# Softplus summed in PSUM, and a part of GpSimd's multiplies given to VectorE, in a selective-scan kernel

## The chip, the cores and the metric

The kernel runs on one core of one Trainium2 chip. The metric is the device time of one execution in microseconds (us). TensorE is called PE in the profile, VectorE DVE, ScalarE ACT, GpSimd POOL and SyncE SP; SP only issues DMAs here.

## The reference, cut to what matters

Two layers work on 16 images of 64 x 64 pixels with 96 channels, in float32. The first is a convolution block (upsample, two matrix multiplies with a quadratic between, low-pass filter). The second, in which the change lies, is a selective scan in four directions over L = 4096 pixels, 192 channels and 16 states:

```python
delta = jax.nn.softplus(dts + dt_bias[None, :, :, None])
...
def step(h, inps):
    dt, ut, bt, ct = inps
    h = jnp.exp(dt[..., None] * As[None]) * h + (dt * ut)[..., None] * bt[:, :, None, :]
    y = jnp.einsum('bkdn,bkn->bkd', h, ct)
    return (h, y)
```

So for each channel and state there is a decay exp(delta A), a drive delta u B, the recurrence h = decay h + drive along the pixels, and a sum of h C over the 16 states.

## The kernel before, in words

All work is issued in an order written out by hand: each engine executes its instructions in the order in which the program emits them, and waits for others by semaphores.

**The main loop** (`scan`, from L833) runs over 3072 units: 16 images x 8 steps (two pairs of directions, four stretches of T = 1024 pixels) x 6 blocks of 64 channels x 4 quarters j of the states. Partitions hold 32 channels x 4 states; each unit has two groups, odd (e = 1) and even (e = 0), of 128 x 1024 elements. A unit n does this:

- `decay(n, e)`, L725: ACT writes da = exp(delta A) to PSUM (two buffers `aps`). It is issued a unit ahead.
- `drive(n)`, L731: POOL writes b = dtu x B for both groups at once into a buffer of the pool `p3` (three of them). It is issued two units ahead.
- `recur(n, e)`, L740 (forward) and L742 (backward): DVE scans h = da h + b. For the odd group the result overwrites b in SBUF, for the even group it overwrites da in PSUM.
- Multiply by C: for the odd group POOL, in place in b (L877); for the even group DVE, from da in PSUM into b (L887).
- `keep(n, e)`, L748: ACT copies the last column of h, 128 x 1, which starts the next stretch. The last stretch of a direction needs none, so there are 2304 copies for each group.
- `read_out(n)`, L764: PE sums b over the states into y in PSUM with sixteen recorded matmuls. It is issued in unit n + 1, so that the buffer b is free for drive(n + 3). At the end of a block `store` (L775) copies y out of PSUM. For the second pair of directions a partial sum y0 is loaded (L702) and added by PE (L757).

In the order of the program a unit is: odd scan, odd keep, odd decay for n + 1, read_out(n - 1), background slot 0, odd multiply on POOL, drive(n + 2) on POOL, even scan, slot 1, even multiply, even keep, even decay for n + 1, slot 2, then loads of B and C (L693).

**Background work** is cut into slices by generators and one slice of each running generator is put into a slot: `project` for the next step (L622), `front` for the next image (the first layer and the convolution, L181), and `finish` for the image before (L510). `project` makes, for each half of 512 pixels and each of three parts v, softplus in the form max(s, 0) + ln(1 + e) with a correction for the rounding of 1 + e, where e = exp(-|s|): in L658 to L674 that is ACT abs, ACT exp, ACT ln, DVE max-add (L664), ACT 1 + e (L666), DVE (1 + e) - 1 - e (L668), DVE subtract (L669), DVE dtu = delta u (L672) and ACT copy of delta (L674); dtu and delta go to DRAM (L676, L677). There are 768 such parts in the run. s lies in the one bank of the PSUM pool `gps`. The blocks load dtu and delta back, spread over the partitions, with `fetch` (L684), each as one tile with both groups and two buffers.

Of the kernel before, what the change touches and what calls it, by code (L numbers as in the profile page):

```python
# [45 lines left out]
F32 = mybir.dt.float32  # L46
AF = mybir.ActivationFunctionType
ALU = mybir.AluOpType
# [3 lines left out]
C = 96  # L52
HW = 64
L = HW * HW
UPS = 100
# [7 lines left out]
T = 1024  # L63
NT = L // T
NQ = 4
QT = T // NQ
TB = 512
# [6 lines left out]
HEAVY = 2  # L74
PSLICES = 60


@with_exitstack
def tile_two_blocks(
# [4 lines left out]
    nc = tc.nc  # L84
# [27 lines left out]
    one_s = const.tile([128, 1], F32, name="one_s")  # L112
    nc.gpsimd.memset(one_s, 1.0)
    eps_g = const.tile([128, 1], F32, name="eps_g")
    nc.gpsimd.memset(eps_g, GEPS)
# [66 lines left out]
    b18 = ctx.enter_context(tc.tile_pool(name="b18", bufs=1))  # L182
    b12 = ctx.enter_context(tc.tile_pool(name="b12", bufs=1))
    b2p = ctx.enter_context(tc.tile_pool(name="b2", bufs=11))
# [55 lines left out]
    def front(mi):  # L240
# [72 lines left out]
        for p0 in range(0, UPS, PP):  # L313
# [93 lines left out]

        JS = 44
        s = [
            b18.tile([UPS, JS, C], F32, name="s0", tag="b18"), b12.tile([UPS, HW - JS, C], F32, name="s1", tag="b12")  # L410
        ]
        for _ in range(2):
            yield
        for i, n, first in [(0, JS // 4, k * JS // 4) for k in range(4)] + [(1, 10, 0), (1, 10, 10)]:
            nc.sync.dma_start(out=s[i][:, first:first + n, :], in_=s_d[:, JS * i + first:JS * i + first + n, :])
            yield
# [3 lines left out]
        done = None  # L420
        for j0 in range(0, HW + 8, 8):
            if done is not None:
                nc.scalar.activation(
                    x1v[:, :, j0 - 8:j0], done.rearrange("c w h -> c h w"), AF.Identity, bias=shift
                )
            if j0 < HW:
                done = bank([C, 8, HW], "e_ps")
                nc.tensor.matmul(
                    done.rearrange("c w h -> c h w"), lhsT=lin, rhs=x1v[:, :, j0:j0 + 8], start=True, stop=False,
                    skip_group_check=True,  # L430
                )
                for j in range(8):
                    nc.tensor.matmul(
                        done[:, j, :], lhsT=s[(j0 + j) // JS][:, (j0 + j) % JS, :], rhs=down_s, start=False, stop=True,
                        skip_group_check=True,
                    )
            yield
# [168 lines left out]
    def scan():  # L606


        with ExitStack() as es:
            pj = es.enter_context(tc.tile_pool(name="sc_pj", bufs=1))  # L610
            up_ = es.enter_context(tc.tile_pool(name="sc_u", bufs=3))
            cp = es.enter_context(tc.tile_pool(name="sc_bc", bufs=5))
            p3 = es.enter_context(tc.tile_pool(name="sc_3", bufs=3))
            p2 = es.enter_context(tc.tile_pool(name="sc_2", bufs=2))
            yp = es.enter_context(tc.tile_pool(name="sc_y", bufs=1))
# [6 lines left out]
            def project(mi, pair, lc, out):  # L622
# [5 lines left out]
                out["dtu"] = [dram.tile([128, T], F32, name=f"dtu_d{v}") for v in range(3)]  # L628
                xs_d = image[mi]["xs"]
                for t in range(0, T, TB):  # L630
                    u = []
                    for v in range(3):
                        uv = up_.tile([128, TB], F32, name="u")
                        nc.sync.dma_start(out=uv, in_=xs_d[v, :, lc * T + t:lc * T + t + TB])
                        u.append(uv)
                    for _ in range(3):
                        yield
                    pp = gps.tile([128, TB], F32, name="pp", tag="g")
                    for v in range(3):
                        nc.tensor.matmul(pp, lhsT=xpt_s[:, pair, v, :], rhs=u[v], start=(v == 0), stop=(v == 2))  # L640
                    yield
                    pr = pj.tile([128, TB], F32, name="pr")
                    nc.scalar.activation(pr, pp, AF.Identity, bias=bumps_s)


                    for i, v in enumerate((0, 2, 1)):
                        if i == 0:
# [8 lines left out]
                        yield  # L656
                        e, d = (pj.tile([128, TB], F32, name=k) for k in ("e", "d"))
                        nc.scalar.activation(e, s, AF.Abs)  # L658
                        nc.scalar.activation(e, e, AF.Exp, scale=-1.0)
                        yield  # L660
                        nc.scalar.activation(d, e, AF.Ln, bias=one_s)
                        for _ in range(2):
                            yield
                        nc.vector.scalar_tensor_tensor(d, s, 0.0, d, ALU.max, ALU.add)  # L664
                        yield
                        nc.scalar.activation(s, e, AF.Identity, bias=one_s)  # L666
                        yield
                        nc.vector.scalar_tensor_tensor(s, s, -1.0, e, ALU.add, ALU.subtract)  # L668
                        nc.vector.tensor_sub(s, d, s)  # L669
                        dtu = pj.tile([128, TB], F32, name="dtu")  # L670
                        delta = pj.tile([128, TB], F32, name="delta")
                        nc.vector.tensor_mul(dtu, s, u[v])  # L672
                        yield
                        nc.scalar.copy(delta, s)  # L674
                        yield
                        nc.sync.dma_start(out=out["dtu"][v][:, t:t + TB], in_=dtu)  # L676
                        nc.sync.dma_start(out=out["delta"][v][:, t:t + TB], in_=delta)  # L677

            def fetch(what, ctx, bi):

                v, s0, r = blocks[bi]
                t = p2.tile([128, 2, T], F32, name=what)
                for e in (1, 0):
                    nc.sync.dma_start(  # L684
                        out=t[:, e, :],
                        in_=ctx[what][v][32 * (s0 + e):32 * (s0 + e) + 32, :].unsqueeze(1).to_broadcast([32, NQ, T]),
                    )
                return t
# [22 lines left out]
            bc = {(what, 0, j): fetch_bc(ctxs[0], 0, j, what) for j in range(NQ) for what in range(2)}  # L711
            ops = {(w, 0): fetch(w, ctxs[0], 0) for w in ("dtu", "delta")}
            y0s, states, ys = {}, [None] * len(blocks), {}
# [8 lines left out]
            def decay(n, e):  # L722
                k, g = group(n, e)
                da = aps.tile([128, T], F32, name="da")
                nc.scalar.activation(da, ops["delta", n // NQ][:, e, :], AF.Exp, scale=a_s[:, k, g, units[n][2]:units[n][2] + 1])  # L725
                das[n, e] = da

            def drive(n):
                b = p3.tile([128, 2, T], F32, name="b")
                bt = bc[0, blocks[units[n][1]][2], units[n][2]]  # L730
                nc.gpsimd.tensor_mul(b, ops["dtu", n // NQ], bt.unsqueeze(1).to_broadcast([128, 2, T]))  # L731
                bs[n] = b
# [10 lines left out]

            def keep(n, e, h):
                st, bi, j = units[n]
                if st % NT < NT - 1:
                    end = h[:, T - 1:T] if steps[st][1] == 0 else h[:, 0:1]
                    nc.scalar.copy(states[bi][1][:, e, j:j + 1], end)  # L748

# [83 lines left out]
            for n, (st, bi, j) in enumerate(units):  # L833
# [19 lines left out]
                if j == 0:  # L853
# [6 lines left out]
                    if ahead:  # L860
                        ops["dtu", m + 1] = fetch("dtu", *ahead)
                elif j == 1:
                    if ahead:
                        ops["delta", m + 1] = fetch("delta", *ahead)
                    if n + NQ <= last and steps[units[n + NQ - 1][0]][1] == 1:
                        st2, bi2, _ = units[n + NQ - 1]
                        y0s[steps[st2][2], bi2] = fetch_y0(steps[st2][2], bi2)

                h = bs[n][:, 1, :]
                recur(n, 1, h)  # L870
                keep(n, 1, h)
                if n < last:
                    decay(n + 1, 1)
                if n:
                    read_out(n - 1)
                slot(0)
                nc.gpsimd.tensor_mul(h, h, bc[1, r, j])  # L877
                if n + 2 <= last:
# [3 lines left out]
                recur(n, 0, h)  # L882
                if n and units[n - 1][2] == NQ - 1:
                    storing = store(n - 1)
                    next(storing)
                slot(1)
                nc.vector.tensor_mul(bs[n][:, 0, :], h, bc[1, r, j])  # L887
                keep(n, 0, h)
                if n < last:
                    decay(n + 1, 0)  # L890
                slot(2)
                if storing is not None:
                    next(storing, 0)
                    storing = None


                at = n % per_step
                for what in range(2):
# [4 lines left out]
                    if 0 <= ahead_j < NQ and st + 1 < len(steps):  # L903
                        bc[what, 0, ahead_j] = fetch_bc(ctxs[st + 1], 0, ahead_j, what)
            read_out(last)
            for _ in store(last):
# [111 lines left out]
```

## Time and profile before

The columns come from the run's times and the page of one profiled execution.

| what | value |
|---|---|
| time, median of 3 runs | 21,918.01 us (21,916.37 to 21,922.08) |
| profiled execution, its own time | 21,910.69 us |
| its span in the profile | 21,908.9 us |
| mean granted TensorE clock | 0.766 of full speed |
| mean DMA rate | 195 GB/s, DMA engines busy 58.1% of the span for the main queue |
| one execution's work | 260,666 instructions |

How to read it: a busy time is the time in which an engine executed something, summed over the span. A share of it is a mean over all stages. In a group of instructions, "mean ns" is the duration of one, and the idle time is that of the engine just before these instructions, with what ended most of it. In the waits, "y L764 <- DVE b L887" means that the instruction on y at line 764 was released last by the DVE instruction at line 887 that wrote b.

### The profile page before, as it was taken

How to read it: one execution, taken by the hardware profiler on the slowest of the kernel's cores; microseconds unless marked ns; L12 is line 12 of the kernel's file. 1: busy time of each engine (PE TensorE's matmuls, PEld its weight loads, DVE VectorE, ACT ScalarE, POOL GpSimd, SP SyncE). 2: the span in 40 equal slices, each digit the busy share in tenths (PEclk: the TensorE clock that was granted, in tenths of full speed). 3: DMA queues.
4: the chain of work that ended last, by engine and by line, in shares of the span. 5: the costliest groups of instructions: out<-in, count | busy, mean ns of one | idle time of the engine just before them, and what ended most of it. 6: DMA issues, size and time to landing. Idle time of an engine off the chain costs nothing.

```text
span 21908.9 us, 260666 instructions
## 1 busy us (share of the span) xinstructions
PE 15342.2 (70%) x92844; PEld 6324.7 (29%) x92844; DVE 19849.9 (91%) x12829; ACT 13130.2 (60%) x20854; POOL 20900.4 (95%) x6152
## 2 busy tenths in 40 slices
PE   6766767766777677777767677767777677677745
PEld 4322323232232322324233232322323223242211
DVE  0999999999999999999999999999999999999996
ACT  4665656666565665656656566665656656566543
POOL 0999999999999999999999999999999999999997
PEclk7776777877778777777877778777787877778856
DMA  2555565656656566565655656556565655656654
GB/s 80 190 191 188 193 214 194 209 195 200 205 191 215 189 206 201 192 215 192 207 198 194 214 192 209 196 201 206 193 211 189 210 199 198 206 195 208 210 177 134
DMA packets 1851895, 4276.30 MB, mean 195 GB/s; under 512 B 449118, under 2 KB 548350, under 8 KB 1848542
## 3 DMA queue, kind: packets, MB, share of 16 engines
q1 hardware_dynamic: 1850590, 4259.62, 58.1%
q8 instruction: 731, 11.98, 0.2%
q14 instruction: 574, 4.70, 0.1%
HBM read 3380.58 MB, written 878.18 MB: 194 GB/s over the span
## 4 chain that ended last, share of the span: by engine, by line
DVE 36%; POOL 19%; issue 18%; PE 9%; ACT 9%; DMA 7%; SPq 1%; POOLq 0%; DVEq 0%; ACTq 0%
POOL b L731 10%; POOL b L877 10%; DVE da L742 7%; DVE da L740 7%; DVE b L740 6%; DVE b L742 6%; DVE b L887 4%; ACT da L725 4%; DMA u<-xs_d 2%; DVE s L669 2%; DVE dtu L672 2%; DVE s L668 2%; PE y L764 1%; DMA ct<-rows 1%; PE pp L640 1%
## 5 line engine op out<-in xcount | busy, mean ns | idle before, releaser
L731 POOL TENSOR_TENSOR b<-dtu,bt 128x2048 f32<-128x2048 f32 x3072 | 13984.9, 4552 | 584.6 <-DMA dtu<-dtu_d 522.9
L725 ACT ACTIVATE da<-delta,a_s 128x1024 f32<-128x1024 f32 x6144 | 6853.5, 1116 | 2826.6 <-DVE b L887 1185.9
L877 POOL TENSOR_TENSOR b<-b,ct 128x1024 f32<-128x1024 f32 x3072 | 7309.1, 2379 | 259.8 <-ACT new L748 249.5
L764 PE MATMUL y<-b,fold_s 128*32 128x256 f32 x49152 | 4638.9, 492 | 4107.3 <-DVE b L887 3102.6
L887 DVE TENSOR_TENSOR b<-da,ct 128x1024 f32<-128x1024 f32 x3072 | 3752.6, 1222 | 84.5
L764 PEld LDWEIGHTS y<-b,fold_s 128*32 128x32 f32 x49152 | 1353.3, 126 | 7627.7 <-DVE b L887 4083.3
L740 DVE TENSOR_TENSOR_SCAN da<-da,new,b 128x1024 f32<-128x1024 f32 x1152 | 2694.3, 2339 | 252.3 <-ACT da L725 252.3
L740 DVE TENSOR_TENSOR_SCAN b<-da,new,b 128x1024 f32<-128x1024 f32 x1152 | 2698.0, 2342 | 174.1 <-POOL b L731 166.9
L742 DVE TENSOR_TENSOR_SCAN da<-da,new,b 128x1024 f32<-128x1024 f32 x1152 | 2693.8, 2338 | 172.9 <-ACT da L725 172.7
L742 DVE TENSOR_TENSOR_SCAN b<-da,new,b 128x1024 f32<-128x1024 f32 x1152 | 2697.1, 2341 | 151.6 <-POOL b L731 109.5
L748 ACT COPY new<-da 128x1 f32<-128x1 f32 x2304 | 362.3, 157 | 3028.5 <-DVE b L887 3023.2
L473 PE MATMUL c_ps<-xgp,wtap_s 96*128 96x512 f32 (+1 forms) x4608 | 1817.8, 675 | 168.9 <-ACT row L491 164.1
L650 PE MATMUL s<-pr,dtw_s 128*128 128x512 f32 x1536 | 1120.4, 819 | 557.8 <-ACT delta L674 516.7
L377 PE MATMUL o_ps<-w2c_s,hsq 128*100 128x96 f32 x9600 | 1205.3, 293 | 191.9 <-ACT hsq L348 180.1
L365 PE MATMUL h_ps<-xu,w1t_s 96*128 96x500 f32 x1920 | 1147.6, 700 | 244.2 <-ACT hsq L348 108.6
L748 ACT COPY new<-b 128x1 f32<-128x1 f32 x2304 | 432.6, 188 | 1445.7 <-DVE b L742 740.4
L377 PEld LDWEIGHTS o_ps<-w2c_s,hsq 128*100 128x100 f32 x9600 | 1119.5, 203 | 407.4 <-ACT hsq L348 227.7
L640 PE MATMUL pp<-u,xpt_s 128*128 128x512 f32 x1536 | 903.7, 734 | 224.2 <-DMA u<-xs_d 216.0
L742 DVE TENSOR_TENSOR_SCAN b<-da,b 128x1024 f32<-128x1024 f32 x384 | 876.7, 2283 | 133.2 <-ACT da L725 74.8
L473 PEld LDWEIGHTS c_ps<-xgp,wtap_s 96*128 96x128 f32 (+1 forms) x4608 | 631.9, 182 | 1193.3 <-issue 938.6
L740 DVE TENSOR_TENSOR_SCAN da<-da,b 128x1024 f32<-128x1024 f32 x384 | 875.8, 2281 | 106.9 <-ACT da L725 106.9
L742 DVE TENSOR_TENSOR_SCAN da<-da,b 128x1024 f32<-128x1024 f32 x384 | 876.0, 2281 | 105.0 <-ACT da L725 105.0
(120 smaller groups left out, 18077.1 us busy)
## 6 DMA issues: line engine op xcount, KB each, us to landing
dtu<-dtu_d SPq DMA_DIRECT2D x1536, 512.0 KB
delta<-delta_d SPq DMA_DIRECT2D x1536, 512.0 KB
bt<-rows SPq DMA_DIRECT2D x1024, 512.0 KB
ct<-rows SPq DMA_DIRECT2D x1024, 512.0 KB
u<-xs_d SPq DMA_DIRECT2D x896, 256.0 KB
dtu_d<-dtu SPq DMA_DIRECT2D x768, 256.0 KB
delta_d<-delta SPq DMA_DIRECT2D x768, 256.0 KB
xr<-in_x SPq DMA_DIRECT2D x768, 128.0 KB
```

The costliest lines, as they stand in the source:

```text
L365: nc.tensor.matmul(h_ps[j], lhsT=w1t_s[:, 128 * j:128 * (j + 1)], rhs=xu.rearrange("c p q -> c (p q)"), start=True, stop=True,)
L377: nc.tensor.matmul(o_ps[:, p, :], lhsT=hsq[j][:, UPS * p:UPS * (p + 1)], rhs=w2c_s[:, j, :], start=(j == 0), stop=(j == HB - 1),)
L473: nc.tensor.matmul(c_ps[p:p + n], lhsT=wtap_s[:, tap, 128 * i:128 * i + n], rhs=xgp[:, h0:h0 + 8, dx:dx + HW], start=(tap == 0), stop=(tap ...
L640: nc.tensor.matmul(pp, lhsT=xpt_s[:, pair, v, :], rhs=u[v], start=(v == 0), stop=(v == 2))
L650: nc.tensor.matmul(s, lhsT=dtw_s[:, pair, v, :], rhs=pr, start=True, stop=True)
L725: nc.scalar.activation(da, ops["delta", n // NQ][:, e, :], AF.Exp, scale=a_s[:, k, g, units[n][2]:units[n][2] + 1])
L731: nc.gpsimd.tensor_mul(b, ops["dtu", n // NQ], bt.unsqueeze(1).to_broadcast([128, 2, T]))
L740: nc.vector.tensor_tensor_scan(out, da, b, before, ALU.mult, ALU.add)
L742: nc.vector.tensor_tensor_scan(out[:, ::-1], da[:, ::-1], b[:, ::-1], before, ALU.mult, ALU.add)
L764: nc.tensor.matmul(y[32 * q:32 * q + 32, e, :], lhsT=fold_s, rhs=b[:, e, QT * q:QT * q + QT], start=(pair == 0 and j == 0 and e == 0), sto ...
L877: nc.gpsimd.tensor_mul(h, h, bc[1, r, j])
L887: nc.vector.tensor_mul(bs[n][:, 0, :], h, bc[1, r, j])
```

## The change

The change has these parts.

- *Softplus in PSUM.* The three DVE operations L664, L668 and L669 and the ACT operation L666 go. ACT makes m = relu(s), w = (1 + e) and w = w - 1 in SBUF tiles; PE adds -w + e + ln(1 + e) + m in PSUM by four matmuls with the identity or its negative (`less_i`). DVE still makes dtu from it, ACT still copies delta.
- *One odd group in five.* For n % 5 = 4 the odd scan writes its result to da in PSUM, and DVE multiplies it by C into b; POOL's multiply is left out there.
- *Odd column copy.* `keep` of the odd group is issued on DVE instead of ACT, except in those fifth units, where ACT copies from da.
- *Read-out.* `read_out(n)` moves from unit n + 1 to unit n + 2, and b has four buffers (`p4`) in place of three; `store` and the load of y0 move along.
- *Loads.* Delta is fetched by halves into three half buffers (odd half at j = 1, even half at j = 2) in place of two whole ones; u has four buffers and is fetched ahead in `project`; the load of s_d in `front` uses one buffer twice (40 and 24 columns) in place of two buffers (44 and 20), which frees room.

```diff
+SHARE = 5
...
+    less_s = const.tile([128, 1], F32, name="less_s")
+    nc.gpsimd.memset(less_s, -1.0)
+    less_i = const.tile([128, 128], F32, name="less_i")
+    nc.vector.tensor_scalar(less_i, ident_s, -1.0, None, ALU.mult)
...
-    b12 = ctx.enter_context(tc.tile_pool(name="b12", bufs=1))
...
-        JS = 44
-        s = [
-            b18.tile([UPS, JS, C], F32, name="s0", tag="b18"), b12.tile([UPS, HW - JS, C], F32, name="s1", tag="b12")
-        ]
+        def fetch_s(first, n):
+            t = b18.tile([UPS, n, C], F32, name="s", tag="b18")
+            for k in range(0, n, 8):
+                nc.sync.dma_start(out=t[:, k:k + 8, :], in_=s_d[:, first + k:first + k + 8, :])
+                yield t, first
+
+        JS = 40
         for _ in range(2):
             yield
-        for i, n, first in [(0, JS // 4, k * JS // 4) for k in range(4)] + [(1, 10, 0), (1, 10, 10)]:
-            nc.sync.dma_start(out=s[i][:, first:first + n, :], in_=s_d[:, JS * i + first:JS * i + first + n, :])
+        for s, s_first in fetch_s(0, JS):
             yield
...
+            if j0 == JS:
+                for s, s_first in fetch_s(JS, HW - JS):
+                    yield
+                for _ in range(2):
+                    yield
...
-            up_ = es.enter_context(tc.tile_pool(name="sc_u", bufs=3))
+            up_ = es.enter_context(tc.tile_pool(name="sc_u", bufs=4))
...
+            p4 = es.enter_context(tc.tile_pool(name="sc_4", bufs=4))
...
+                order = (0, 2, 1)
+
+                def fetch_u(v, t):
+                    uv = up_.tile([128, TB], F32, name="u")
+                    nc.sync.dma_start(out=uv, in_=xs_d[v, :, lc * T + t:lc * T + t + TB])
+                    return uv
+
+                ahead_u = [fetch_u(v, 0) for v in order]
+                for _ in range(4):
+                    yield
...
-                        e, d = (pj.tile([128, TB], F32, name=k) for k in ("e", "d"))
+                        e, d, m, w = (pj.tile([128, TB], F32, name=k) for k in ("e", "d", "m", "w"))
                         nc.scalar.activation(e, s, AF.Abs)
                         nc.scalar.activation(e, e, AF.Exp, scale=-1.0)
                         yield
+                        nc.scalar.activation(m, s, AF.Relu)
+                        nc.scalar.activation(w, e, AF.Identity, bias=one_s)
+                        yield
                         nc.scalar.activation(d, e, AF.Ln, bias=one_s)
+                        nc.scalar.activation(w, w, AF.Identity, bias=less_s)
+                        yield
+                        s = gps.tile([128, TB], F32, name="s", tag="g")
+                        yield
+                        for k, (sign, of) in enumerate(((less_i, w), (ident_s, e), (ident_s, d), (ident_s, m))):
+                            nc.tensor.matmul(s, lhsT=sign, rhs=of, start=(k == 0), stop=(k == 3))
                         for _ in range(2):
                             yield
-                        nc.vector.scalar_tensor_tensor(d, s, 0.0, d, ALU.max, ALU.add)
-                        yield
-                        nc.scalar.activation(s, e, AF.Identity, bias=one_s)
-                        yield
-                        nc.vector.scalar_tensor_tensor(s, s, -1.0, e, ALU.add, ALU.subtract)
-                        nc.vector.tensor_sub(s, d, s)
...
+                        if t + TB < T:
+                            ahead_u.append(fetch_u(v, t + TB))
...
-                b = p3.tile([128, 2, T], F32, name="b")
+                b = p4.tile([128, 2, T], F32, name="b")
...
-            def keep(n, e, h):
+            def keep(n, e, h, copy):
...
-                    nc.scalar.copy(states[bi][1][:, e, j:j + 1], end)
+                    copy(states[bi][1][:, e, j:j + 1], end)
...
                 elif j == 1:
                     if ahead:
-                        ops["delta", m + 1] = fetch("delta", *ahead)
-                    if n + NQ <= last and steps[units[n + NQ - 1][0]][1] == 1:
-                        st2, bi2, _ = units[n + NQ - 1]
-                        y0s[steps[st2][2], bi2] = fetch_y0(steps[st2][2], bi2)
-
-                h = bs[n][:, 1, :]
+                        deltas[m + 1, 1] = fetch_delta(*ahead, 1)
+
+                odd_here = n % SHARE == SHARE - 1
+                h = das[n, 1] if odd_here else bs[n][:, 1, :]
                 recur(n, 1, h)
-                keep(n, 1, h)
+                if odd_here:
+                    nc.vector.tensor_mul(bs[n][:, 1, :], h, bc[1, r, j])
+                keep(n, 1, h, nc.scalar.copy if odd_here else nc.vector.tensor_copy)
                 if n < last:
                     decay(n + 1, 1)
-                if n:
-                    read_out(n - 1)
+                if j == 2 and ahead:
+                    deltas[m + 1, 0] = fetch_delta(*ahead, 0)
+                if n >= 2:
+                    read_out(n - 2)
                 slot(0)
-                nc.gpsimd.tensor_mul(h, h, bc[1, r, j])
+                if not odd_here:
+                    nc.gpsimd.tensor_mul(h, h, bc[1, r, j])
...
-                if n and units[n - 1][2] == NQ - 1:
-                    storing = store(n - 1)
+                if n >= 2 and units[n - 2][2] == NQ - 1:
+                    storing = store(n - 2)
...
+                if j == NQ - 1 and n < last and steps[units[n + 1][0]][1] == 1:
+                    st2, bi2, _ = units[n + 1]
+                    y0s[steps[st2][2], bi2] = fetch_y0(steps[st2][2], bi2)
```

## The prediction

> **What bounds the kernel now.** I read the first page of the profile, then the groups of instructions by line and shape, the table of who waited for whom, the timeline of a few units in mid-run, and a table of stages. A "unit" below is one turn of the main loop (one block, one quarter j); there are 3072. First the page: span and busy time.
>
> ```profile
> span 21908.9 us, 260666 instructions
> PE 15342.2 (70%) x92844; PEld 6324.7 (29%) x92844; DVE 19849.9 (91%) x12829; ACT 13130.2 (60%) x20854; POOL 20900.4 (95%) x6152
> ```
>
> POOL (GpSimd) and DVE (VectorE) are nearly full. The timeline of one undisturbed unit (start, duration, engine, line, tiles) shows which sets the pace:
>
> ```profile
> 10015.91 2.35 POOL L877 TENSOR_TENSOR b<-b,ct 128x1024 f32<-128x1024 f32 x1
> 10016.86 2.34 DVE L740 TENSOR_TENSOR_SCAN b<-da,new,b 128x1024 f32<-128x1024 f32 x1
> ...
> 10018.22 4.53 POOL L731 TENSOR_TENSOR b<-dtu,bt 128x2048 f32<-128x2048 f32 x1
> ...
> 10019.12 2.33 DVE L740 TENSOR_TENSOR_SCAN da<-da,new,b 128x1024 f32<-128x1024 f32 x1
> ...
> 10021.49 1.23 DVE L887 TENSOR_TENSOR b<-da,ct 128x1024 f32<-128x1024 f32 x1
> 10022.63 0.68 DVE L664 SCALAR_TENSOR_TENSOR d<-s,d 128x512 f32<-128x512 f32 x1
> 10022.70 2.37 POOL L877 TENSOR_TENSOR b<-b,ct 128x1024 f32<-128x1024 f32 x1
> ```
>
> POOL goes 2.31 + 4.48 = 6.79 us from L877 to the next L877 with no gap. DVE's fixed part is 2.26 + 2.37 + 1.14 = 5.77 us; softplus and other small work come on top. So POOL is the bound: 3072 x 6.79 = 20,859 us. The waits (total, times, longest) say what else there is:
>
> ```profile
> PE y L764 <- DVE b L887: 3102.6, 1248, 33.7
> ...
> POOL b L731 <- DMA dtu<-dtu_d: 522.9, 9, 512.3
> ...
> DVE da L740 <- ACT da L725: 359.2, 285, 5.9
> ...
> POOL b L877 <- ACT new L748: 249.5, 168, 4.0
> ```
>
> POOL starts at 512 us (first image's front and projection). Its other idle time is (584.6 - 512.3) + 259.8 = 332 us, by the two group rows; 250 of it waits for ACT's column copy L748. What is left of the span, 21,909 - 512 - 20,859 - 332 = 206 us, is the last image's finish. Groups by line and shape, with count, busy us, mean ns and idle:
>
> ```profile
> L731 POOL TENSOR_TENSOR b<-dtu,bt 128x2048 f32<-128x2048 f32 x3072 | 13984.9, 4552 | 584.6 <-DMA dtu<-dtu_d 522.9 <-PE y L764 15.9 <-DMA rows<-pr 12.0
> L877 POOL TENSOR_TENSOR b<-b,ct 128x1024 f32<-128x1024 f32 x3072 | 7309.1, 2379 | 259.8 <-ACT new L748 249.5 <-DMA delta_d<-delta 0.6 <-DMA dtu_d<-dtu 0.5
> L887 DVE TENSOR_TENSOR b<-da,ct 128x1024 f32<-128x1024 f32 x3072 | 3752.6, 1222 | 84.5
> L640 PE MATMUL pp<-u,xpt_s 128*128 128x512 f32 x1536 | 903.7, 734 | 224.2 <-DMA u<-xs_d 216.0 <-ACT da L725 4.7 <-ACT new L748 3.5
> L669 DVE TENSOR_TENSOR s<-d,s 128x512 f32<-128x512 f32 x768 | 534.5, 696 | 26.2
> L236 DVE TENSOR_TENSOR nb<-nmean,rg 96x1 f32<-96x1 f32 x32 | 27.3, 855 | 293.3 <-ACT rg L233 293.3
> L259 DVE TENSOR_TENSOR lin<-lin,ident_s 96x96 f32<-96x96 f32 x16 | 19.4, 1215 | 0.0
> ```
>
> The stage table (stretch, length, busy us of PE, its weight loads, DVE, ACT, POOL, then granted TensorE clock, DMA share, GB/s), one stretch of the convolution, one of finish, one with little background work:
>
> ```profile
> 9265.00:9330.00 65.00, 51.28 (x252) 16.87 (x256) 59.74 (x37) 44.33 (x65) 63.68 (x20) 0.82 0.65 235
> ...
> 9590.00:9655.00 65.00, 55.66 (x225) 16.36 (x218) 64.62 (x44) 36.17 (x62) 63.82 (x20) 0.81 0.62 206
> ...
> 9785.00:9850.00 65.00, 26.81 (x172) 6.75 (x164) 58.00 (x35) 32.40 (x58) 65.00 (x20) 0.58 0.61 204
> ```
>
> PE is 79% to 86% busy in the two heavy stretches; keep that for the rivals.
>
> **What the Trainium skill says.** (1) "SBUF — State Buffer", section "SBUF: two separate sides": VectorE and GpSimd share one port pair as an exclusive lock, and VectorE needs it with two SBUF inputs or in a two-port mode. The trace agrees: L259, both inputs in SBUF, takes 245 ns before POOL has started and 1278 ns (median) later; L258 beside it, one input in PSUM, keeps 125 ns. So the odd multiply, whose h lies in PSUM, should not contend. (2) "Advanced Engine Details and Errata", section "VectorE Performance Modes": the two-port mode needs an even outermost dimension, or odd and above 1. By that a 128x1 copy stays on one port. No run here shows it. (3) "TensorE: Matmul & The Clock Gate", Part 1: activity releases the clock's throttle. The stages agree: 0.58 at 41% busy, 0.81 at 86%.
>
> **The change part by part.**
>
> *Odd multiply.* Where n % 5 is 4, L877 goes from POOL: 614 x 2.31 = 1,418 us less, POOL's work 20,859 - 1,418 = 19,441. DVE gets 614 x 1.222 = +750 (row L887: same shape, one operand in PSUM). Scan then writes to da in PSUM, which the even scan does already at the same 2.34.
>
> *Softplus.* L664, L668, L669 leave DVE: (674 + 679 + 696 ns) x 768 = -1,574 (the first two from their rows in the same table). dtu stays. ACT loses one activation (L666, 673 ns) and gains relu (like L658, 582) and two identities (about 673 each): +1.255 x 768 = +964. PE gains four 128x512 matmuls per part, 3072 in all; row L640 gives 903.7 / 768 = 1.18 us per matmul (two records each), so about +3,620 us: 15,342 becomes some 18,960. They lie beside POOL and DVE, if PE keeps up.
>
> *Column copy.* Odd columns were 2304 ACT copies at 188 ns; 1843 (four in five) go to DVE, the rest stay. ACT loses 346, so with softplus it stands at about 13,750, 69% of the new span. On DVE the copy must await the scan, so the 0.08 us by which the records of two scans overlap is lost, then comes a start gap of 0.03 (as before L887) and the copy. Lower bound: 0.06 as the short memset at L169 (59 ns). Upper bound: a copy that meets POOL's lock, up to 1.32 as the longest L236. I take 0.09 for the copy itself, between that memset and L258, and 0.20 with the gaps: +369. Queued behind it are the even scan and its multiply, and POOL's L877 waits for it in place of ACT: the 250 us of POOL idle there goes.
>
> DVE's sum: 19,850 + 750 - 1,574 + 369 = 19,395. POOL has 19,441. Each is about 6.32 us per unit: the two are balanced, and neither has slack.
>
> *Read-out a pair later, four b buffers.* The distance from read_out to the drive that reuses the buffer stays within one unit in the program, but PE no longer waits for data of the unit just computed: nearly all of y's 3,103 us on L887 can go, which is where the new matmuls can fit. Zero by itself; if that cover is missing, see rival 1.
>
> *Delta in three half buffers, u fetched ahead, s in one buffer.* Delta's second half is issued at j = 2 behind the decay that frees it and is due 1.7 units (10.7 us) later. Waits for DMA in before are 10.6 us in all past the start, so I take 0; bounds 0 and +2 us x 768 = 1,500. u ahead saves PE's 216 us on u, off the path. Three loads of s now stand behind reads of the same buffer, with five more turns for the loads: about four slices of 540 more per image, inside the slack in which 9785 to 9850 runs bare. Zero. Bounds for these edits apart from delta: -50 and +100. SP moves u, y0 and delta within a unit or so; each still waits for things that come before it in program order.
>
> *Start.* The first projection is bare: per part +0.58 + 0.67 + 0.67 + 4.7 for ACT and PE, -0.67 for L666, -2.05 for DVE, so +3.9, six times: +23.
>
> *Stalls.* With POOL at 6.79 and DVE at 6.44 POOL lost 332. Now lateness of either hurts. DVE's waits for decays (359 on L740's da, 278 and 115 on L742's rows) were nearly free and are no longer: 752. Bounds 80 (332 less the copy's 250) and 1,100; I take 650, near the sum of these waits, some of which go with ACT's copies.
>
> Sum against the profiled execution: 512 + 23 + 19,441 + 650 + 206 = 20,832, from a span of 21,909 (execution 21,910.7; the median of the runs shown is 7 us or 0.03% above). Forecast: 20,830 us, -5.0%.
>
> **Rivals.** *1, PE becomes the bound.* For: 86% busy in finish, one more matmul of 1.18 us per unit against a unit that shrinks to 6.3. Busy 18,960 / 3072 = 6.17 per unit, plus about 0.6 of waits for ACT (2,300 us of PE idle not due to y, part of which stays) = 6.77: with the 741 us of start and finish 3072 x 6.77 + 741 = 21,540. Against: the clock rises with activity, and 1.18 holds a clock near 0.77. *2, the balance holds without stalls.* 512 + 23 + 19,441 + 80 + 206 = 20,260. For: four b buffers. Against: two engines at 100% with lumps of 0.7 us on DVE. *3, slower: the 128x1 copy takes the shared port.* If each of the 1843 copies waits as L259 does (1278 - 245 = 1.03 us) the copy costs 1.23 with its gaps, DVE has 19,395 + 1,900 = 21,295, and with 650 of stalls the time is 741 + 21,295 + 650 = 22,690. It decides from 1,120 us of waits (0.61 per copy), 21,909 less 741, 650 and 19,395. For: L236, a 96x1 operation, was hit. Against: that has two SBUF inputs, the copy one.
>
> **How the numbers follow.** Forecast 0.57, rival 1 0.24 (four fifths of it below 21,800), rival 2 0.07, rival 3 with late deltas 0.12. The forecast's own range is 20,450 to 21,150; to leave out no more than 2 in 10 the range goes from 20,400 to 21,650. The measurement tells about 0.2% from no change: faster 0.85, same 0.02, slower 0.13.
>
> **What would show it.** Right: POOL near 19,480 busy with 2458 multiplies, gaps of 3% between; DVE near 19,400; the copy at 60 to 130 ns; y on PE hardly waiting for DVE; granted clock above 0.80. Wrong: copies of 0.5 us or more; POOL waiting for PE's y or ACT for delta's DMA in hundreds of us; PE over 93% busy at the old clock.

## The result, and the profile after

The changed kernel takes 22,628.13 us (median of 4 runs, 22,614.26 to 22,653.19) against 21,917.19 for the kernel before (4 runs, 21,914.62 to 21,922.08): ratio 1.0325, 95% interval 1.0307 to 1.0343. It is 711 us slower, where 1,088 us less than the 21,918 of the runs shown was forecast. The page's two lines first: span, and busy time of each engine.

```profile
span 22651.4 us, 273692 instructions
...
PE 17130.4 (76%) x98988; PEld 7369.8 (33%) x98988; DVE 19487.5 (86%) x12984; ACT 13765.2 (61%) x20546; POOL 19514.3 (86%) x5539
```

The work did move as planned: POOL fell from 20,900 to 19,514 us, DVE from 19,850 to 19,488. But no engine is near full any more: POOL went from 95% to 86%. So what was lost was lost in idle time. Where, the groups by line and shape tell (count, busy us, mean ns, then idle time of the engine just before, with its causes):

```profile
L761 POOL TENSOR_TENSOR b<-dtu,bt 128x2048 f32<-128x2048 f32 x3072 | 13894.0, 4529 | 2267.9 <-PE y L794 1364.8 <-DMA dtu<-dtu_d 544.3 <-issue 230.8
...
L910 POOL TENSOR_TENSOR b<-b,ct 128x1024 f32<-128x1024 f32 x2458 | 5792.4, 2357 | 704.3 <-DVE new L778 430.8 <-DVE b L770 105.3 <-issue 90.6
...
L687 PE MATMUL s<-w,less_i 128*128 128x512 f32 x1536 | 1161.9, 847 | 950.0 <-ACT w L682 839.5 <-ACT new L778 109.9
...
L656 PE MATMUL pp<-u,xpt_s 128*128 128x512 f32 x1536 | 1142.0, 881 | 1184.8 <-DMA u<-xs_d 1135.3 <-ACT delta L693 49.0
...
L900 DVE TENSOR_TENSOR b<-da,ct 128x1024 f32<-128x1024 f32 x614 | 752.1, 1225 | 45.9 <-PE y L787 0.4 <-issue 0.4
...
L679 ACT ACTIVATE w<-e,one_s 128x512 f32<-128x512 f32 x768 | 547.3, 713 | 0.0
...
L778 DVE COPY new<-b 128x1 f32<-128x1 f32 x1844 | 283.8, 154 | 63.1
```

Take 543 us, POOL's longest wait, which is the start, from the two POOL rows: 2,268 + 704 - 543 = 2,429 us of idle time past the start. Before it was 332; the forecast had 650. The largest cause, 1,365 us, is one that was 16 us before: the drive at L761 waits until PE has read a b buffer (y L794). PE in turn stood still for two things of its own: 1,135 us before the matmul on pp, for the load of u, and 840 us before the first matmul of the new sum, for ACT's w. The waits of the same kernel (total, times, longest) put them in order:

```profile
POOL b L761 <- PE y L794: 1364.8, 455, 16.6
...
PE pp L656 <- DMA u<-xs_d: 1135.3, 219, 23.9
...
PE s L687 <- ACT w L682: 839.5, 298, 8.7
...
DVE da L770 <- ACT da L755: 829.0, 427, 18.4
...
DVE dtu L692 <- PE s L687: 692.2, 280, 137.6
...
PE y L794 <- DVE b L920: 484.0, 123, 9.9
...
POOL b L910 <- DVE new L778: 430.8, 295, 6.6
```

The last but one was 3,103 us before: PE hardly waits for DVE's multiply any more, as forecast. The "longest" column matters for the first lines: POOL waits of 16.6 us and DVE waits of 18.4 us are more than two units long (a unit takes 22,651 / 3072 = 7.4 us here). The timeline shows a place with one of the longest waits for u; the mean of the 219 is 1,135 / 219 = 5.2 us (start, duration, engine, line, operation, in brackets the idle time before and what ended it):

```profile
8012.22 0.67 DVE L692 TENSOR_TENSOR dtu<-s,u 128x512 f32<-128x512 f32 x1
...
8014.02 1.13 PE L656 MATMUL pp<-u,xpt_s 128*128 128x512 f32 x2 [1.12 <-ACT delta L693]
...
8019.71 0.35 SPq L695 DMA_DIRECT2D dtu_d<-dtu  x1
...
8021.65 0.34 SPq L696 DMA_DIRECT2D delta_d<-delta  x1
...
8023.19 0.32 SPq L646 DMA_DIRECT2D u<-xs_d  x1
...
8031.23 3.78 PE L656 MATMUL pp<-u,xpt_s 128*128 128x512 f32 x4 [16.08 <-DMA u<-xs_d]
...
8035.06 0.69 ACT L660 ACTIVATE pr<-pp,bumps_s 128x512 f32<-128x512 f32 x1 [15.23 <-PE pp L656]
...
8039.38 4.52 POOL L761 TENSOR_TENSOR b<-dtu,bt 128x2048 f32<-128x2048 f32 x1 [15.85 <-PE y L794]
...
8043.38 2.36 DVE L770 TENSOR_TENSOR_SCAN da<-da,new,b 128x1024 f32<-128x1024 f32 x1 [17.62 <-ACT da L755]
```

Read it downward. The last part of the first half ends with dtu at 8012.89. PE begins the next half's pp with the first of its three matmuls (x2 are its two records). The second reads the tile that was asked for last: its load comes to SP's turn only at 8023.19, behind the two stores, and its data releases PE at 8031.23, 8.04 us later. So half of the wait is SP's late turn, and half is the load itself. In those 16.08 us PE executes nothing, since it goes in order; ACT, whose next instruction is the read of pp, stands 15.23 us; the decays behind it are late, and DVE stands 17.62; PE's read-outs are late, so no b buffer comes free, and POOL stands 15.85. One late load of 256 KB stops four engines.

### The profile page after: what moved, and what is told of

Same layout as the page of the kernel before. It is cut to its first block, busy times and chain, and to the rows that moved or that the text cites. A ratio compares the mean times of both kernels' runs of the same rounds, so it can differ in the third digit from the quotient of the medians.

```text
span 22651.4 us, 273692 instructions
## 1 busy us (share of the span) xinstructions
PE 17130.4 (76%) x98988; PEld 7369.8 (33%) x98988; DVE 19487.5 (86%) x12984; ACT 13765.2 (61%) x20546; POOL 19514.3 (86%) x5539
## 5 line engine op out<-in xcount | busy, mean ns | idle before, releaser
L761 POOL TENSOR_TENSOR b<-dtu,bt 128x2048 f32<-128x2048 f32 x3072 | 13894.0, 4529 | 2267.9 <-PE y L794 1364.8
L910 POOL TENSOR_TENSOR b<-b,ct 128x1024 f32<-128x1024 f32 x2458 | 5792.4, 2357 | 704.3 <-DVE new L778 430.8
L794 PE MATMUL y<-b,fold_s 128*32 128x256 f32 x49152 | 3786.5, 434 | 705.9 <-DVE b L920 484.0
L770 DVE TENSOR_TENSOR_SCAN da<-da,new,b 128x1024 f32<-128x1024 f32 x1383 | 3246.9, 2348 | 680.2 <-ACT da L755 678.4
L772 DVE TENSOR_TENSOR_SCAN da<-da,new,b 128x1024 f32<-128x1024 f32 x1382 | 3243.3, 2347 | 248.9 <-ACT da L755 238.4
L794 PEld LDWEIGHTS y<-b,fold_s 128*32 128x32 f32 x49152 | 1405.0, 119 | 3412.3 <-issue 1445.6
L772 DVE TENSOR_TENSOR_SCAN b<-da,new,b 128x1024 f32<-128x1024 f32 x922 | 2158.3, 2341 | 158.7 <-ACT da L755 145.9
L770 DVE TENSOR_TENSOR_SCAN b<-da,new,b 128x1024 f32<-128x1024 f32 x921 | 2156.5, 2341 | 67.8 <-ACT da L755 66.2
L656 PE MATMUL pp<-u,xpt_s 128*128 128x512 f32 x1536 | 1142.0, 881 | 1184.8 <-DMA u<-xs_d 1135.3
L687 PE MATMUL s<-w,less_i 128*128 128x512 f32 x1536 | 1161.9, 847 | 950.0 <-ACT w L682 839.5
L667 PE MATMUL s<-pr,dtw_s 128*128 128x512 f32 x1536 | 901.9, 670 | 544.2 <-ACT delta L693 310.7
L772 DVE TENSOR_TENSOR_SCAN da<-da,b 128x1024 f32<-128x1024 f32 x461 | 1056.3, 2291 | 173.1 <-ACT da L755 170.4
L770 DVE TENSOR_TENSOR_SCAN da<-da,b 128x1024 f32<-128x1024 f32 x460 | 1053.6, 2290 | 156.1 <-ACT da L755 150.7
L692 DVE TENSOR_TENSOR dtu<-s,u 128x512 f32<-128x512 f32 x768 | 525.5, 684 | 698.9 <-PE s L687 692.2
L687 PE MATMUL s<-e,ident_s 128*128 128x512 f32 x1536 | 1033.8, 763 | 0.0
```

The costliest lines, as they stand in the source:

```text
L687: nc.tensor.matmul(s, lhsT=sign, rhs=of, start=(k == 0), stop=(k == 3))
L761: nc.gpsimd.tensor_mul(b, dtus[n // NQ], bt.unsqueeze(1).to_broadcast([128, 2, T]))
L770: nc.vector.tensor_tensor_scan(out, da, b, before, ALU.mult, ALU.add)
L772: nc.vector.tensor_tensor_scan(out[:, ::-1], da[:, ::-1], b[:, ::-1], before, ALU.mult, ALU.add)
L794: nc.tensor.matmul(y[32 * q:32 * q + 32, e, :], lhsT=fold_s, rhs=b[:, e, QT * q:QT * q + QT], start=(pair == 0 and j == 0 and e == 0), sto ...
```

## The experiments

Each was measured beside the kernel before on the same chip. Where an interval is given the kernel ran 4 to 6 times; the others were timed once, so a difference of a few tens of us between them carries no weight. "Idle" below is POOL's idle time past the start, from its two group rows, as above.

**The u loads.** After, with the loads of the second half asked for one part earlier:

```diff
                     for _ in range(2):
                         yield
+                    if t + TB < T:
+                        ahead_u.append(fetch_u(order[0], t + TB))
...
-                        if t + TB < T:
-                            ahead_u.append(fetch_u(v, t + TB))
+                        if t + TB < T and i < 2:
+                            ahead_u.append(fetch_u(order[i + 1], t + TB))
```

> The changed kernel, with each load of u for the second half of a step issued one part earlier (the first behind the matmuls on pp, the second and third behind the first and second part), so that none stands in the same slice as the matmul that reads it. Theory U (PE, in order, stands still at L656 until a load issued just before it has landed, 937 us in the 128 second halves of the changed kernel, and the read-outs behind it hold up GpSimd): PE's wait for u falls below 350 us, POOL's wait for y below 600 us, and the time falls by 700 to 950 us to about 21,700 to 21,900. Rival P (the 3072 added matmuls make PE late wherever they stand): the time stays above 22,400.

Measured: 21,839.42 us (21,833.66 to 21,845.65), 789 less than after; against before 0.9966, interval 0.9954 to 0.9979. The waits of this kernel:

```profile
POOL b L763 <- PE y L796: 668.5, 350, 8.9
...
PE pp L656 <- DMA u<-xs_d: 255.7, 95, 24.5
```

PE's wait for u falls from 1,135 to 256 us, POOL's longest wait for y from 16.6 to 8.9, its idle from 2,429 to 1,618: 811 less, which accounts for the 789 of time. PE's wait and the time came as theory U had them; POOL's whole wait for y, 669 us, stayed above its 600. Where the loads are placed turns the change from 3.2% slower to 0.3% faster.

The reverse, the change's u loads alone put into before (four u buffers, the loads at the end of each part, four slices ahead of the first half and none ahead of the second):

> The kernel before with the change's loads of u alone (four buffers, the third load for the second half in one slice with the matmul that reads it). Theory U: PE waits for u by some 900 us instead of 216, and with the read-out only one unit behind the time rises by 300 to 900 us, to 22,200 to 22,800. Rival P: within 100 us of the kernel before.

Measured: 22,393.12 us, 478 more than before, by itself: in theory U's range, though PE's wait for u is 588 us and not some 900. The wait in question, and POOL's drive:

```profile
PE pp L644 <- DMA u<-xs_d: 588.3, 129, 13.4
...
L738 POOL TENSOR_TENSOR b<-dtu,bt 128x2048 f32<-128x2048 f32 x3072 | 13933.6, 4536 | 1003.1 <-DMA dtu<-dtu_d 516.0 <-issue 349.9 <-DMA rows<-pr 35.5
```

129 times is about one for each second half, of which there are 16 images x 8 steps = 128. POOL's idle rises from 332 to 813 us, 481 more, which accounts for the 478. The trace names no releaser for 350 of it ("issue"); at 8,251 us, for one, such a wait of 3.26 us ends right behind PE's read-outs L771, which had stood behind a wait of 5.34 us for u.

**The softplus.** Before, with the new softplus alone:

```diff
-                        nc.vector.scalar_tensor_tensor(d, s, 0.0, d, ALU.max, ALU.add)
...
+                        for k, (sign, of) in enumerate(((less_i, w), (ident_s, e), (ident_s, d), (ident_s, m))):
+                            nc.tensor.matmul(s, lhsT=sign, rhs=of, start=(k == 0), stop=(k == 3))
```

> The kernel before with softplus added up in PSUM and nothing else of the change. DVE loses 1,574 us of work, PE gains 3072 matmuls, POOL's work stays at 20,859. Theory U: POOL still sets the time, 21,700 to 22,000. Rival P: PE's lateness holds up the read-outs, above 22,200.

Measured: 22,378.21 us, 464 more than before, though DVE's work fell to 18,561 us: POOL was the bound, and its idle went from 332 to 755. So theory U's range is missed and rival P's met. But P's path, late read-outs, carries little of it: POOL's wait for y is 109 us. More of it stands behind ACT's column copies, and DVE waits longer for ACT's decays:

```profile
DVE da L746 <- ACT da L731: 719.8, 530, 6.3
...
POOL b L883 <- ACT new L754: 452.2, 292, 5.3
```

Before, these were 359 and 250 us.

The opposite, the e1 kernel with the softplus of before on DVE:

> The changed kernel with u earlier as in e1, but softplus on DVE as in the kernel before. DVE's sum is then 19,488 + 1,574 = about 21,060 busy, so DVE is the bound: 21,060 + 741 + 400 to 800 of stalls = 22,200 to 22,600 by theory U, slower than e1. Rival P: PE is relieved, so it is faster than e1.

Measured: 22,379.99 us. Its busy line:

```profile
PE 15260.6 (68%) x92844; PEld 6536.5 (29%) x92844; DVE 20911.9 (93%) x15288; ACT 13004.9 (58%) x19010; POOL 19511.3 (87%) x5539
```

Here DVE is the bound. So the softplus has to leave DVE for the other parts to pay; what is in question is the form in which it does.

**Is the sum issued too late?** e1 with the sum one slice sooner after its last input, and three slices from there to dtu:

```diff
                         s = gps.tile([128, TB], F32, name="s", tag="g")
-                        yield
                         for k, (sign, of) in enumerate(((less_i, w), (ident_s, e), (ident_s, d), (ident_s, m))):
...
-                        for _ in range(2):
+                        for _ in range(3):
                             yield
```

> e1 with the four matmuls of the softplus sum issued one slice sooner, and three slices in place of two between them and dtu. Theory S (what is left over the forecast comes from the sum's time on PE: about 4.5 us in one piece, against some 4.3 us that two slices give, so DVE stands at dtu and what follows is late): DVE's wait for s falls below 300 us from 676 (136 of them at the start), the time falls by 150 to 400 us to 21,440 to 21,690. Rival B (the rest is lost evenly because POOL and DVE are both full, through waits for decays and column copies): within 80 us of e1's 21,839.

Measured: 21,910.87 us, 71 more than e1. Its waits:

```profile
PE s L688 <- ACT w L684: 1448.1, 471, 8.3
...
POOL b L762 <- PE y L795: 1072.1, 491, 8.9
...
DVE dtu L693 <- PE s L688: 340.8, 195, 137.8
```

DVE waits half as long for the sum (676 in e1), PE longer for ACT's w (923), and POOL longer for PE (669): the wait was moved to another place, and the gain of theory S did not come.

The other way, slack on both sides (relu, 1 + e, ln and w - 1 in one slice, two slices to the sum, three to dtu):

> e1 with ACT's relu, 1 + e, ln and w - 1 in one slice, two slices then until the sum and three from the sum to dtu; the number of slices stays. Theory H1: PE's wait for w falls from 923 us below 600 and DVE's wait for s below 350, and the time to 21,350 to 21,700. Theory H2: the sum's length is what costs, the time stays within 120 us of 21,839.

Measured: 21,836.08 us, 3 less than e1. POOL's wait for y is 871, DVE's for the sum 320, PE's for w 833, which theory H1 had below 600. Moving the slices does not win the time back; the next runs leave some of the work out.

**The length of the softplus.** e1 without the two rounding terms, that is, with the sum of ln(1 + e) and m alone:

```diff
-                        nc.scalar.activation(w, e, AF.Identity, bias=one_s)
-                        nc.scalar.activation(w, w, AF.Identity, bias=less_s)
...
-                        for k, (sign, of) in enumerate(((less_i, w), (ident_s, e), (ident_s, d), (ident_s, m))):
+                        for k, (sign, of) in enumerate(((ident_s, d), (ident_s, m))):
```

> e1 without the rounding correction of softplus: the two terms w and e are left out of the sum, with ACT's two operations on w, so PE has 1536 matmuls fewer and ACT 1,090 us less; what is computed is ln(1 + e) + max(s, 0) only. Theory S: the sum is half as long and ready sooner, DVE's wait for s nearly goes, the time falls by 400 to 800 us to 21,040 to 21,440. Rival B: above 21,600.

Measured: 21,068.49 us, 771 less than e1; idle falls from 1,618 to 887. To divide this between ACT (two operations) and PE (two of four matmuls), e9 keeps four matmuls but sums -e + e, so that ACT's two operations go:

```diff
-                        for k, (sign, of) in enumerate(((less_i, w), (ident_s, e), (ident_s, d), (ident_s, m))):
+                        for k, (sign, of) in enumerate(((less_i, e), (ident_s, e), (ident_s, d), (ident_s, m))):
```

> e1 with all four matmuls in the sum, but e in the place of w, so that ACT's two operations on w go (1,090 us of ACT) and PE keeps its length; the rounding correction of softplus is left out (its two terms cancel). It splits the 771 us by which e6 was faster than e1. Theory H1 (PE stands at the sum because ACT makes w late, and ACT is late for the decays): near e6, 21,050 to 21,350. Theory H2 (the length of the sum on PE, some 4.5 us in one piece, delays the read-outs behind it and dtu): near e1, 21,550 to 21,850.

Measured: 21,351.48 us: ACT's two operations, with PE's wait for their result, account for 488 of the 771, the two matmuls for 283. And e13 puts the two operations back into e9 with nothing that reads w, so that ACT works as long and PE does not stand for it:

> e9 with ACT's two operations on w put back, their result read by nobody (the sum takes e twice, so the rounding correction is left out). ACT's load is that of e1, PE's wait for w is not there. If ACT's load is what costs: near e1, 21,700 to 21,880. If PE's standing at the sum for w is what costs: near e9, 21,300 to 21,500.

Measured: 21,727.92 us. ACT's time alone costs 21,728 - 21,351 = 376 us, PE's standing for w the remaining 111. POOL's rows, first of e9, then of e13:

```profile
L761 POOL TENSOR_TENSOR b<-dtu,bt 128x2048 f32<-128x2048 f32 x3072 | 13894.0, 4529 | 1033.9 <-DMA dtu<-dtu_d 513.2 <-PE y L794 426.0 <-issue 53.6
...
L910 POOL TENSOR_TENSOR b<-b,ct 128x1024 f32<-128x1024 f32 x2458 | 5792.8, 2357 | 640.4 <-DVE new L778 342.0 <-DVE b L770 93.1 <-issue 73.0
```

```profile
L763 POOL TENSOR_TENSOR b<-dtu,bt 128x2048 f32<-128x2048 f32 x3072 | 13905.8, 4534 | 1194.6 <-PE y L796 559.6 <-DMA dtu<-dtu_d 512.9 <-issue 66.4
...
L912 POOL TENSOR_TENSOR b<-b,ct 128x1024 f32<-128x1024 f32 x2458 | 5803.0, 2361 | 847.5 <-DVE new L780 476.6 <-issue 143.6 <-DVE b L772 101.7
```

Both of POOL's waits grow, that for PE's y (426 to 560) and that for DVE's column (342 to 477). DVE waits longer for ACT's decays too; the largest of these waits, of e9 and of e13:

```profile
DVE da L770 <- ACT da L755: 332.5, 293, 5.0
```

```profile
DVE da L772 <- ACT da L757: 454.6, 400, 5.9
```

So the decays come later, DVE's scans with them, and what is behind the scans. ACT is 60% busy in e9 and 63% in e13. Its two operations, 1.42 us per part by their rows (886 us in all by the busy lines, in which overlapping records count once), are not work in spare time, since in order they stand ahead of decays that are due.

**The column copy.** e1 with the odd copy on ACT again:

```diff
-                keep(n, 1, h, nc.scalar.copy if odd_here else nc.vector.tensor_copy)
+                keep(n, 1, h, nc.scalar.copy)
```

> e1 with the odd column copy back on ACT in all units. DVE loses 1844 copies of 154 ns with their gaps (about 350 us), POOL's multiply waits for ACT instead of DVE. Theory S: DVE is not what binds where the time is lost, so the time changes by -100 to +250 us. Rival B: DVE's 350 us are worth 150 to 350 us, to 21,490 to 21,690.

Measured: 21,753.90 us, 85 less than e1, and 162 less than before, with the same computation. The wait for the copy more than doubles, yet the kernel is faster:

```profile
POOL b L912 <- ACT new L780: 989.2, 590, 6.5
```

It was 458 from DVE in e1; in exchange POOL's wait for y falls from 669 to 322, and DVE has 260 us less to do.

**The share.** e1 with all odd multiplies on POOL (`SHARE = 10 ** 6`):

> e1 with all odd multiplies on POOL again. POOL's work is 20,859 and with start and finish 21,600; DVE loses 750 and has 8 percent to spare. Theory S: the lateness of PE and ACT stays, so the time rises by 200 to 500 us to 22,040 to 22,340. Rival B: with DVE's slack back the stalls shrink to some 300 and the time is about 21,900, within 100 us of e1.

Measured: 22,034.21 us, 118 more than before and 195 more than e1. POOL's busy time is 20,900 against 19,521 in e1, but its idle is 434 against 1,618. Giving 1,379 us of POOL's work away brings 195, since 1,184 return as idle.

**The read-out.** e1 with `read_out(n - 1)` and three b buffers, as before:

> e1 with read_out in the next unit again, three b buffers, and y0 and store moved along. Theory H (what is left over the forecast is PE's lateness at the softplus sum, and the read-outs behind it hold b): with one unit less of room the wait of POOL for y grows beyond 1,000 us and the time to 22,150 to 22,700, as in e3. Rival (the read-out's distance does nothing by itself, as the prediction priced it): 21,740 to 21,940.

Measured: 21,835.39 us, 4 from e1. PE's wait for DVE's multiply at y grows from 483 to 1,954 us, and the time stays; PE's wait for u falls from 256 to 49 at the same time, so "nothing" is the sum of both.

**Both findings together.** e10 is e6 with the copy on ACT; so it too leaves out the correction for the rounding of 1 + e. With the correction kept, the fastest run here is e7.

> The two terms of e6 and the odd column copy on ACT of e7 together (the rounding correction of softplus is left out). If the two add up: 21,068 - 85 = about 20,980, between 20,900 and 21,080. If POOL's wait for ACT's copy, 989 us in e7, takes the place of the wait for PE: above 21,100.

Measured: 20,930.07 us (20,910.52 to 20,938.08); ratio to before 0.9545, interval 0.9529 to 0.956. Its busy line and its two POOL groups:

```profile
PE 15884.8 (76%) x95916; PEld 6795.5 (32%) x95916; DVE 19156.3 (92%) x11140; ACT 13048.1 (62%) x20854; POOL 19504.6 (93%) x5539
```

```profile
L761 POOL TENSOR_TENSOR b<-dtu,bt 128x2048 f32<-128x2048 f32 x3072 | 13901.8, 4534 | 689.2 <-DMA dtu<-dtu_d 517.8 <-PE y L794 144.8 <-issue 9.6
...
L910 POOL TENSOR_TENSOR b<-b,ct 128x1024 f32<-128x1024 f32 x2458 | 5806.1, 2362 | 571.9 <-ACT new L778 480.6 <-DVE b L770 62.8 <-DVE b L772 20.2
```

POOL has the work that it has in after, 19,505 against 19,514, and 743 us of idle in place of 2,429. The time between follows: 22,651 - 20,932 = 1,719 by the spans.

**Delta by halves.** e10 with delta loaded whole, as before:

```diff
-            def fetch_delta(ctx, bi, e):
-                t = p3.tile([128, T], F32, name="delta")
-                spread(t, "delta", ctx, bi, e)
+            def fetch_delta(ctx, bi):
+                t = p2.tile([128, 2, T], F32, name="delta")
+                for e in (1, 0):
+                    spread(t[:, e, :], "delta", ctx, bi, e)
...
-                        deltas[m + 1, 1] = fetch_delta(*ahead, 1)
+                        deltas[m + 1] = fetch_delta(*ahead)
...
-                if j == 2 and ahead:
-                    deltas[m + 1, 0] = fetch_delta(*ahead, 0)
```

> e10 with delta fetched as in the kernel before: both halves at j = 1 into one of two whole buffers (less_i, which e10 does not read, is left out to make room). If the fetch in halves costs nothing, as the prediction priced it: within 80 us of e10's 20,930. If SyncE's waits for the decays make other loads late: 150 us or more below, 20,780 or less.

Measured: 20,924.54 us, 6 from e10: no effect.

**The account.** POOL's idle from after to e10, one step at a time: u loads 2,429 - 1,618 = 811 (e1); the two rounding terms 1,618 - 887 = 731 (e6); the copy 887 - 743 = 144 (e10); left 743. The single steps are shown for this order of removal; e7 against e1 and e10 against e6 show that in time the copy on ACT is worth 85 with the rounding terms and 138 without, so the steps are not strictly independent.

## Why the prediction was wrong

The forecast was 20,832 us of execution; the profiled span is 22,651. Of the difference of 1,819 us, POOL's idle accounts for 2,429 - 650 = 1,779, its busy time for 19,514 - 19,441 = 73; start and finish nearly cancel (544 and 165 us against 535 and 206).

- *Amounts of work: right.* POOL 19,514 (19,441 forecast), DVE 19,488 (19,395), odd multiply on DVE 1,225 ns (1,222), ACT 13,765 (13,750). The balance came about as computed; it does not set the time. (Two figures on the way are misread: 13,750 is 66% of the forecast span and not 69%, and the 10.6 us "in all" of waits for DMA are those of POOL's drive alone; PE's 216 us for u come on top.)
- *"u ahead saves PE's 216 us, off the path": the step that failed most.* It was read as a load moved ahead. For two of three tiles it is; the third is asked for at the end of the third part, and the next instruction of the generator is the matmul that reads it, with no slice between. PE's wait went from 216 to 1,135 us, and off the path it was not: e1 takes most of this wait away and 789 us of time with it. The prediction's own sign of being wrong, POOL waiting for PE's y in hundreds of us, came with 1,365. The bounds of -50 and +100 missed 811 us of idle. The diff alone showed this: three slices between load and use were removed ahead of the second half, and none was put back.
- *Softplus: "They lie beside POOL and DVE, if PE keeps up": the second step that failed.* Busy times were right and the price of nothing was wrong. ACT's two operations on w cost 488 us (376 by their own length, 111 by PE's wait for w) and two of PE's matmuls 283, in engines that are 63% and 78% busy in e1. The condition was put on PE's total ("6.17 per unit"), where it should have been put on what stands in order behind these instructions: read-outs behind four matmuls, decays behind ACT's three new operations. That the decays are late is shown (e13); by which wait the two matmuls cost their 283 us was not taken apart.
- *Stalls of 650: mis-sized for the change, near for what is left.* It was 2,429; without the two causes above, and with the copy on ACT, e10 has 743. The forecast priced the loss of slack for waits that were in before, and none for waits that the change makes.
- *Column copy: its sum near by luck, wrong in its sign.* The copy takes 154 ns where 90 was forecast, and the idle time before it is 63 us in all, 0.03 per copy, where 0.11 was set for gaps and lost overlap: the two errors nearly cancel, 347 us against 369. POOL does not hold it up. But of the 250 us of POOL's wait that it was to remove, the DVE form shows 431 in after, and the ACT form is 85 to 138 us better.
- *Read-out and delta at nothing: right* (e11, e14). That y's wait for DVE would vanish was right too (3,103 to 484), but that the new matmuls need this gap was not: e11 has the wait and the same time.
- *Rival 1, PE as the bound.* PE was forecast 18,960 busy and has 17,130. It is not full. What it names is near, though: PE's order, not its sum, is what holds up POOL in after. *Rival 3* gives almost the measured time, 22,690, and falls: its copies were to cost over half a microsecond more each, and took 154 ns.

Open: the same u loads cost 478 us in before and some 800 in after, where PE also waits longer for them (1,135 against 588 us); what makes the difference was not tried. The load of s_d through one buffer and the fourth u buffer were not tried by themselves. The 743 us of idle left in e10 were not taken apart, and delta by halves was tried in e10 only. The division 376, 111 and 283 rests on kernels timed once.

## What to carry to other kernels

When two engines are brought to balance and both near full, ask of each instruction added on a third engine what stands behind it in that engine's order, and not whether that engine has idle time left: here 2 of ACT's operations and 2 of PE's matmuls per part, in engines at 63% and 78%, cost 771 us. A prefetch is worth the number of slices between its issue and its first reader, so count them for each tile and each turn of the loop, the last one above all. And a part of a change may be worth little while another spoils it: with the u loads mended, and the other stalls still there, the share gained 195 of its 1,379 us.

## What the runs showed of the hardware that was not expected

The TensorE clock follows the work: 0.766 before, 0.838 after, 0.756 with the u loads alone (e2), 0.841 with the softplus alone (e3). The 3,072 new matmuls take 3,888 us by their four group rows, yet PE's busy time rose by 1,788 only. Part of this is counting: the busy line counts overlapping records once, and all of PE's group rows together rose by 2,341 (16,015 to 18,356). For the rest, the other matmuls became shorter, by 1,546 us together; the read-outs L794 alone took 4,639 us before and 3,787 after. Two stretches of after, with busy us of PE, weight loads, DVE, ACT and POOL, then clock, DMA share and GB/s, show both ends:

```profile
9590.00:9655.00 65.00, 62.09 (x291) 25.45 (x290) 52.67 (x38) 49.87 (x68) 59.41 (x18) 1.00 0.51 162
...
10175.00:10240.00 65.00, 36.89 (x172) 12.65 (x168) 57.50 (x40) 42.40 (x83) 59.41 (x18) 0.62 0.57 177
```

At 96% busy PE has its full clock, at 57% it has 0.62. The Trainium skill, "TensorE: Matmul & The Clock Gate", Part 1, says that activity releases the throttle, and all these figures agree. The forecast's error fits this: it kept the old matmuls at their old length, and had 18,960 us of PE where 17,130 came.

The 128x1 copy from b on VectorE takes 154 ns (153 to 157 in all 1,844), less than the same copy on ScalarE (186 in e7, 188 before), beside a GpSimd that is 86% busy. The 1.03 us by which L259 grew beside GpSimd is in none of them. This agrees with the single port that the skill's "Advanced Engine Details and Errata", section "VectorE Performance Modes", leads one to expect for such a copy, which no run had shown when the forecast was made.
